# Four graph layers on 32 graphs: constants' set-up behind the first loads, zero fills and tables among the batches' operations, the last two batches' ends side by side

## The chip, the core and the metric

The kernel runs on one core of one Trainium2 chip, as one launch. The metric is the device time in microseconds (us). A core has five engines that run their own streams in order and meet at semaphores: TensorE (PE; its weight loads are listed as PEld), VectorE (DVE), ScalarE (ACT), GpSimd (POOL) and SyncE (SP), which issues the DMAs of the kernel before. Times of instructions come from a profile of one execution and are counted from the start of its span.

## The reference

The input `x` is 32 graphs of 512 nodes with 64 channels, `adj` is 32 weighted adjacency matrices of 512 by 512 in float32. Four layers follow each other, each with a residual and a layer norm:

```python
x = _layernorm(x + _L0_gnn_ref(x, adj), axis=-1)      # (A / deg) @ x
x = _layernorm(x + _L1_gnn_ref(x, adj, ...), axis=-1) # Chebyshev polynomials of the Laplacian, order 4
x = _layernorm(x + _L2_gnn_ref(x, adj, ...), axis=-1) # attention in hyperbolic space over all pairs of nodes
x = _layernorm(x + _L3_gnn_ref(x, adj, nodemask, ...), axis=-1)
```

The last layer thins the neighbours out (`_dilate_adj`), takes for each node and channel a weighted mix of the 0.25, 0.5 and 0.75 quantiles of its neighbours' values, and ends in a small network:

```python
sv = jnp.sort(vals, axis=2)            # neighbours' values, sorted for each channel
...
    q = gather(lo) * (1.0 - frac) + gather(hi) * frac
    agg = agg + wt * q
...
out = (1.0 + EPS_GIN) * x + agg
h = jax.nn.relu(jnp.einsum('bnc,ch->bnh', out, W1) + b1)
y = jnp.einsum('bnh,ho->bno', h, W2) + b2
return y * mask[..., None].astype(dtp)
```

## The kernel before

A batch is one graph; nodes are tiled as T = 4 tiles of P = 128 rows, D = 64 channels. The work of a batch is cut into lanes, each a function that records its operations: `front` (layers 0 and 1: four loads of the matrix as tiles `front_A`, transposes into `front_AT`, products), `pairs` (layer 2's pairwise part, tiles `EX`, `RW`, `Q`), `tail` (the end of layer 2 up to `x3`, sent to DRAM as `xs`), `graph` (the thinned matrix, ranks of the nodes by degree `rk`, slots of the neighbours), `gather` (the neighbours' values by one-hot products into the planes `SB` and `SH`), `sort` (a sorting network on `SB` for nodes from rank 32 on, then the products with the rank tables, collected in the PSUM tile `PA` and copied to `ap`), and, once for two batches, `head` (the network on `SH` for the first 32 ranks of both batches, sums in `PRS`).

`head` ends with `finish` for the one batch and then for the other. `finish` takes ranks back to nodes: it transposes `rk` (4 products with the identity), copies the result to `rr`, builds four one-hot tiles `PT` with two ACT operations each (`onehot`: an Abs with a bias into `dist`, then a Relu), multiplies `ap` by them, adds `x3`, and calls `dense`: two ACT copies (`oT`, `hT`) around the product with `w1s`, four pairs of products with `onesb` and `w2s`, then on DVE the mask and the residual, a layer norm (DVE statistics, a power on POOL, four ACT operations) and the DMA to `out`. The tiles `rr`, `oT`, `hT`, `zo` have one buffer and the lane has one PSUM bank `head_bank`, so that the second batch's end follows the first's.

The order is not that of the code. While `seq.on` is set, the class `Order` only records operations with costs written out by hand; `issue` (line 294) then plans them with due times by lane (`STAGES`) and tile buffers, and emits each engine's stream in the planned order. Where the plan leaves a gap on PE, it fills it with matmuls that compute nothing needed (`stay_active`, lines 1376 to 1379, into `PA`), one for each 0.11 us of the planned gap. They are real instructions: the stream runs through them whether the gap is there or not.

```python
if e == "PE":

    for _ in range(int((t - spare - fill) / 0.11)):
        before[e] = self.pin(filler(), before.get(e))
```

Ahead of this, the constants are set up in the usual way (lines 506 to 667): masks and index rows by POOL and DVE, eleven small loads and then the node mask on SP's queue (lines 589 to 643), products for folded weights into the PSUM pool `ps_0`. The masks' tile `nm` and the row `ii` share memory with tiles allocated later, so their users wait for one another. The table `tabs` is zeroed by POOL (line 555), filled by four DVE copies (lines 557 and 574). `SB`, `SH` and `PRS` are zeroed by POOL (lines 1368, 1369 and 1371). `PA` (line 1374) uses memory of `ps_0` and waits for the set-up's last product's copy, `b1f` (line 665). The first loads of the matrix stand behind the constants' loads on SP.

If a flag says that the degrees lie outside the planned bounds, a slow path (from line 1538) recomputes layer 3; it is not taken with these inputs.

Of the kernel before, what the change touches and what calls it, by code (L numbers as in the profile page):

```python
# [8 lines left out]
F32 = mybir.dt.float32  # L9
# [393 lines left out]
def tile_adj_resnorm(ctx: ExitStack, tc: tile.TileContext, x, adj, nodemask, w1k, b1k, att_w, att_b,  # L403
# [16 lines left out]
    pools = {}  # L420

# [79 lines left out]
    def bank(dtype=F32):  # L501
        return seq.tile(pools["ps"], [P, 512 if dtype == F32 else 1024], dtype, "bank", bufs=BANKS.get(seq.lane, 2))


# [20 lines left out]
    with tc.tile_pool(name="first", bufs=1) as first:  # L525
        ii = first.tile([P, N], I32, name="ii")
        nc.gpsimd.iota(ii, pattern=[[1, 2], [2, H2]], base=0, channel_multiplier=0)
        nc.vector.tensor_copy(iotap, ii)
# [21 lines left out]
    nc.vector.tensor_copy(kf, ks)  # L550
    tb = const.tile([P, K], F32, name="tb")
    ts(tb, kf, part, PAD, op0=OP.is_ge, op1=OP.mult)

    tabs = const.tile([P, K, P], F16, name="tabs")
    nc.gpsimd.memset(tabs, 0.0)
    for h in range(2):
        nc.vector.tensor_copy(tabs[h * HM:(h + 1) * HM, :, h * D:(h + 1) * D],
                              tb[h * HM:(h + 1) * HM].unsqueeze(2).to_broadcast([HM, K, D]))
    PADS, RANKS = slice(0, 2 * HM), slice(2 * HM, P)
    acc = const.tile([P, K], F32, name="acc")  # L560
    nc.vector.memset(acc, 0.0)
    tn = const.tile([P, K], F32, name="tn")
    tau = const.tile([P, 1], F32, name="tau")
    for q, w in TAUS:
        ts(tau, part, -1.0, q, op0=OP.add, op1=OP.mult)
        ts(tau, tau, 0.0, None, op0=OP.max)
        ts(tb, kf, tau, None, op0=OP.subtract)
        ts(tn, tb, -1.0, None, op0=OP.mult)
        tt(tb, tb, tn, op=OP.max)
        ts(tb, tb, -1.0, 1.0, op0=OP.mult, op1=OP.add)  # L570
        ts(tb, tb, 0.0, w, op0=OP.max, op1=OP.mult)
        tt(acc, acc, tb, op=OP.add)
    for h in range(2):
        nc.vector.tensor_copy(tabs[(h + 2) * HM:(h + 3) * HM, :, h * D:(h + 1) * D],
                              acc[(h + 2) * HM:(h + 3) * HM].unsqueeze(2).to_broadcast([HM, K, D]))
# [13 lines left out]
    nc.sync.dma_start(wk[:, :, :D], w1k.rearrange("k u c o -> (k u c) o").rearrange("(g p) o -> p g o", p=P))  # L589
    def rows(src, n, name, m):  # L590
        t = const.tile([m, n], F32, name=name)
        nc.sync.dma_start(t, bass.AP(tensor=src.tensor, offset=src.offset, ap=[[0, m], [1, n]]))
        return t

    def parts3(src, name):

        rem, n = src, src.shape[-1]
        full = const.tile([3, n], F32, name=name + "s")
        part3 = const.tile([3, n], BF16, name=name + "p")
# [12 lines left out]
    b1f = const.tile([3, D + 2], F32, name="b1f")  # L612
    nc.sync.dma_start(b1f[:, :D], bass.AP(tensor=b1k.tensor, offset=b1k.offset, ap=[[0, 3], [1, D]]))
    attb = rows(att_b, 1, "attb", P)
    bias2 = parts3(rows(b2, D, "b2f", 3), "bias2")
    meanf = const.tile([D, D], F32, name="meanf")
    nc.vector.memset(meanf, 1.0 / D)
    attw = const.tile([D, 2], F32, name="attw")
    for k in range(2):
        nc.sync.dma_start(attw[:, k:k + 1], bass.AP(tensor=att_w.tensor, offset=att_w.offset + (1 - k) * D, ap=[[1, D], [1, 1]]))  # L620
    b1c = const.tile([D, 1], F32, name="b1c")
    nc.sync.dma_start(b1c, bass.AP(tensor=b1k.tensor, offset=b1k.offset, ap=[[1, D], [1, 1]]))

    wt = const.tile([P, D], F32, name="wt")
# [8 lines left out]
    for h in range(2):  # L633
        nc.sync.dma_start(w1s[h * D:(h + 1) * D], w1)
    b1s = const.tile([HID, 1], F32, name="b1s")
    nc.sync.dma_start(b1s, b1.rearrange("(h u) -> h u", u=1))
    w2s = const.tile([HID, D], F32, name="w2s")
    nc.sync.dma_start(w2s, w2)

    nmask = const.tile([P, T, B], F32, name="nmask")  # L640
    with tc.tile_pool(name="ps_0", bufs=1, space=PSUM) as ps, tc.tile_pool(name="masks", bufs=1) as masks:
        nm8 = masks.tile([B, N], U8, name="nm8")
        nc.sync.dma_start(nm8, nodemask)
        nmf = masks.tile([B, N], F32, name="nmf")
# [10 lines left out]
        wkT = const.tile([D, P], F32, name="wkT")  # L655
# [573 lines left out]
    def head(b, res):  # L1229
# [22 lines left out]
        for g in range(2):  # L1252
            finish(b - 1 + g, res["ends"][g], ap[:, g])

    def finish(b, end, ap):
        rk, x3 = end
        pt = bank()
# [17 lines left out]
    def dense(po, x3T, x3, dst, nm):  # L1275

        fin = pools["fin"]
        oT = seq.tile(fin, [P, N], F32, "oT", 1)
# [5 lines left out]
        ph = bank()  # L1284
        mm(ph[:HID, :], w1s, oT, start=True, stop=True)
        hT = seq.tile(fin, [HID, N], F32, "hT", 1)
        act(hT, ph[:HID, :], AF.Relu, bias=b1s)
        py = bank()[:, :T * D].rearrange("p (t n) -> p t n", n=D)
# [3 lines left out]
        z = wide("zo")  # L1292
# [12 lines left out]
    gi = const.tile([P, B], I32, name="gi")  # L1305
    nc.gpsimd.iota(gi, pattern=[[-T, B]], base=0, channel_multiplier=1)
    gf = const.tile([P, B], F32, name="gf")
# [4 lines left out]
    def within_bounds():  # L1312
# [17 lines left out]
        for i, op in enumerate((OP.is_gt, OP.is_lt)):  # L1330
# [7 lines left out]

    STAGES = {"front": (-0.6, 0.2), "pairs": (1.2, 1.3), "tail": (0.2, 1.5), "graph": (0.9, 1.0), "gather": (2.7, 2.9),
              "sort": (4.5, 4.6), "head": (4.7, 5.6), "check": (3.1, 4.9)}

    nc.scalar.preload_act_table_set("natural_log_exp_and_others")
    with ExitStack() as fast:
        def pool(name, bufs, **kw):
            pools[name] = fast.enter_context(tc.tile_pool(name=name, bufs=bufs, **kw))
        pool("loads", 2)
# [4 lines left out]
        pool("keep", 2)  # L1353
        pool("oh", 2)
        pool("S", 1)
        pool("fin", 1)
# [9 lines left out]
        nc.gpsimd.memset(FLS[:, :, :, D + 1:D + 2], 1.0)  # L1366
        nc.gpsimd.memset(FLS[:, :, :, NL - 4:NL - 3], 1.0)
        nc.gpsimd.memset(SB, 0.0)
        nc.gpsimd.memset(SH, 0.0)
        PRS = pools["S"].tile([P, 2 * CUT * NR], F32, name="PRS")  # L1370
        nc.gpsimd.memset(PRS, 0.0)

# [250 lines left out]
```

## Time and profile before

| | |
|---|---|
| runs before | 2675.84, 2677.36, 2685.98 us; median 2677.36 us |
| profiled execution | 2680.23 us, span 2678.4 us |
| PE busy | 2514.1 us (94%), fillers among it |
| DVE busy | 2493.2 us (93%) |
| ACT busy | 1854.6 us (69%) |
| POOL busy | 352.9 us (13%) |
| DVE busy from 320 to 400 us | 79.10 of 80 us |
| DVE busy from 40 to 60 us | 6.59 of 20 us |
| DVE busy from 2640 to 2660 us | 2.07 of 20 us |
| mean granted TensorE clock | 0.98 |

The busy shares are averages over a start in which the lanes fill up, a long middle in which every batch goes through the same stream, and an end in which only the last two batches are left. In a list of the timeline, a line has the start in us, the length of the group in us, the engine, the source line, the operation, the output and inputs with their shapes, how many instructions were merged, and in brackets the idle time before it with what ended it. In the chain of waits a line has start, length, engine, tile or line.

### The profile page before, as it was taken

How to read it: one execution, taken by the hardware profiler on the slowest of the kernel's cores; microseconds unless marked ns; L12 is line 12 of the kernel's file. 1: busy time of each engine (PE TensorE's matmuls, PEld its weight loads, DVE VectorE, ACT ScalarE, POOL GpSimd, SP SyncE). 2: the span in 40 equal slices, each digit the busy share in tenths (PEclk: the TensorE clock that was granted, in tenths of full speed). 3: DMA queues.
4: the chain of work that ended last, by engine and by line, in shares of the span. 5: the costliest groups of instructions: out<-in, count | busy, mean ns of one | idle time of the engine just before them, and what ended most of it. 6: DMA issues, size and time to landing. Idle time of an engine off the chain costs nothing.

```text
span 2678.4 us, 55594 instructions
## 1 busy us (share of the span) xinstructions
PE 2514.1 (94%) x19764; PEld 1657.7 (62%) x19793; DVE 2493.2 (93%) x10191; ACT 1854.6 (69%) x4264; POOL 352.9 (13%) x329
## 2 busy tenths in 40 slices
PE   7999999999999999999999999999999999999988
PEld 5666566666666665665666666666566566666556
DVE  5689999999999999999999999999999999999993
ACT  2666768677677767777777776768767677776642
POOL 2111111111101111111111111111211111110100
PEclk9999999999999999899999999999999999999999
DMA  1100000000000000000000000000000000000000
GB/s 37 31 25 21 13 17 19 23 21 25 19 17 11 21 25 21 23 19 7 23 21 25 19 23 13 15 23 21 23 21 19 9 21 25 19 9 3 7 5 8
DMA packets 119721, 49.96 MB, mean 19 GB/s; under 512 B 53740, under 2 KB 119436, under 8 KB 119436
## 3 DMA queue, kind: packets, MB, share of 16 engines
q1 hardware_dynamic: 119436, 46.34, 6.5%
q8 instruction: 157, 2.57, 0.4%
q14 instruction: 128, 1.05, 0.1%
HBM read 37.93 MB, written 8.39 MB: 17 GB/s over the span
## 4 chain that ended last, share of the span: by engine, by line
DVE 74%; PE 18%; POOL 3%; ACT 2%; issue 2%; DMA 0%; POOLq 0%; DVEq 0%; ACTq 0%
DVE SB L445 17%; DVE SH L445 10%; DVE gather_oh L449 7%; PE front_bank L488 4%; DVE pairs_Q L445 3%; PE gather_bank L488 3%; PE pairs_bank L488 3%; DVE pairs_RW L445 3%; DVE pairs_Wt L452 2%; DVE pairs_L L452 2%; PE graph_bank L488 2%; PE head_bank L488 2%; DVE sort_prod L445 2%; DVE tail_v L445 2%; DVE pairs_EX L452 1%
## 5 line engine op out<-in xcount | busy, mean ns | idle before, releaser
L445 DVE TENSOR_TENSOR SB<-SB 128x448 f32<-128x448 f32 (+11 forms) x1424 | 573.6, 426 | 11.0
L488 PE MATMUL gather_bank<-gather_oh,tail_x3h 128*64 128x448 f16 (+2 forms) x5376 | 537.4, 332 | 4.3 <-ACT SB L469 3.7
L488 PEld LDWEIGHTS <-tail_x3h 128*64 128x64 bf16 x5376 | 303.2, 111 | 210.3 <-issue 107.9
L445 DVE TENSOR_TENSOR SH<-SH 128x128 f32<-128x128 f32 (+11 forms) x1744 | 358.3, 248 | 6.5
L488 PE MATMUL pairs_bank<-pairs_FT 67*128 67x512 f32 (+7 forms) x768 | 319.5, 519 | 19.6 <-DVE pairs_EX L452 13.8
L449 DVE TENSOR_SCALAR gather_oh<-graph_slot 128x256 f16<-128x256 f16 (+4 forms) x864 | 264.0, 352 | 10.7 <-PE gather_bank L488 10.6
L488 PE MATMUL front_bank<-front_AT,front_y 128*64 128x512 f32 x768 | 200.3, 615 | 13.0 <-DVE front_y L445 11.4
L694 POOL TENSOR_TENSOR front_rs<-front_var,mhalf 128x4 f32<-128x4 f32 x64 | 79.8, 1248 | 944.1 <-DVE front_var L449 815.8
L488 PEld LDWEIGHTS pairs_bank<-pairs_FT 67*128 67x128 f32 (+1 forms) x768 | 127.2, 195 | 78.4 <-DVE pairs_EX L452 22.2
L488 PEld LDWEIGHTS <-graph_nbT 128*128 128x128 f16 x1536 | 113.2, 99 | 82.0 <-DVE graph_do L452 23.5
L488 PE MATMUL PA<-identf,sort_prod 128*128 128x128 f32 (+4 forms) x960 | 151.0, 288 | 3.2 <-DVE sort_prod L445 2.5
L488 PE MATMUL graph_bank<-graph_perm,graph_V 128*128 128x512 f16 x512 | 135.9, 380 | 2.3 <-DVE graph_perm L449 2.0
L488 PEld LDWEIGHTS PA<-identf,sort_prod 128*128 128x128 f32 (+4 forms) x960 | 118.1, 173 | 26.7 <-issue 16.5
L488 PEld LDWEIGHTS pairs_bank<-FLS,pairs_Wt 128*128 128x128 f32 x1024 | 125.2, 192 | 14.6 <-DVE pairs_Wt L452 5.7
L469 ACT ACTIVATE graph_VP<-graph_bank 128x512 f16<-128x512 f32 x128 | 75.8, 592 | 76.8 <-PE graph_bank L488 76.2
L488 PE MATMUL pairs_bank<-FLS,pairs_Wt 128*128 128x66 f32 x1024 | 126.2, 273 | 2.0 <-DVE pairs_Wt L452 1.8
L488 PEld LDWEIGHTS front_bank<-XA,front_AT 128*128 128x128 f32 x1024 | 120.7, 192 | 9.2 <-ACT front_AT L469 3.0
L488 PE MATMUL front_bank<-XA,front_AT 128*128 128x65 f32 x1024 | 120.5, 273 | 0.8 <-ACT front_AT L469 0.6
L488 PE MATMUL head_bank<-head_PT,sort_ap 128*64 128x512 f32 x256 | 119.6, 616 | 0.6 <-ACT head_PT L469 0.6
L469 ACT ACTIVATE pairs_L<-pairs_L,pairs_oo 128x512 f32<-128x512 f32 x128 | 90.7, 719 | 40.9 <-DVE pairs_L L452 40.3
L469 ACT ACTIVATE graph_v<-graph_bank,graph_c 128x512 f16<-128x512 f32 x128 | 87.0, 680 | 43.0 <-PE graph_bank L488 22.6
L488 PE MATMUL graph_bank<-UC,graph_nbT 128*128 128x512 f16 (+3 forms) x512 | 93.7, 304 | 20.9 <-DVE graph_do L452 18.4
(327 smaller groups left out, 6169.4 us busy)
## 6 DMA issues: line engine op xcount, KB each, us to landing
front_A<-in_adj_dram SPq DMA_DIRECT2D x128, 256.0 KB, 2.8
XA<-in_x_dram SPq DMA_DIRECT2D x32, 128.0 KB, 2.2
xs<-tail_x SPq DMA_DIRECT2D x32, 128.0 KB, 2.0
out_dram<-head_zo SPq DMA_DIRECT2D x32, 128.0 KB, 2.0
wk<-in_L_gnn_weight_dram SPq DMA_DIRECT2D x1, 64.0 KB, 2.1
w1s<-in_L_gnn_W_dram SPq DMA_DIRECT2D x2, 32.0 KB, 2.2
attw<-in_L_gnn_att_W_dram SPq DMA_DIRECT2D x2, 0.2 KB, 2.3
w2s<-in_L_gnn_W_dram SPq DMA_DIRECT2D x1, 32.0 KB, 2.5
```

Source lines behind the costliest of these rows:

```text
L445: vec(lambda: nc.vector.tensor_tensor(out, a, b, op=op), out, [a, b])
L449: vec(lambda: nc.vector.tensor_scalar(out, a, s1, s2, op0=op0, **kw), out, [a], True, (s1, s2))
L452: vec(lambda: nc.vector.scalar_tensor_tensor(out, a, s, b, op0=op0, op1=op1), out, [a, b], False, (s,))
L469: 0.3, lambda: nc.scalar.activation(out, a, f, scale=scale, **kw), [out, accum_out], [a, after] + sc, table)
L488: return nc.tensor.matmul(out, w, a, start=start, stop=stop)
L694: seq.op("POOL", 0.8, 0.6, lambda: nc.gpsimd.tensor_tensor(y, v, mhalf, op=OP.pow), [y], [v])
```

## The change

1. The constants' loads are issued from ACT's queue in place of SP's, so that SP begins with the batches' loads. Set-up tiles that nothing later needs go into a pool `first` that is closed before the fast pools open, and the fast pools are opened in another order (`fin`, `oh`, `keep` first).
2. `SB`, `SH`, `PRS` and `tabs` are zeroed by ACT (a copy of a column of ones, scaled by 0, 768 columns at a time), and the tables are computed, as recorded operations in lane `gather` of batch 0; the four DVE copies into `tabs` become ACT copies.
3. The last two batches have their one-hot tiles built beforehand, in a lane `ends` of their own, in the memory of `EX` and `RW`; the last batch's end gets its own tiles (`ends`, in the memory of `Q`, and a column tile of lane `tail`) and the bank of lane `pairs`.

The streams of the built programs differ at their beginning and from the last batches' `gather` on; between them each engine's instructions stand in the same order in both. On PE the fillers behind each of the first four groups of transposes are 18, 18, 13 and 18 (12 each before); the 33 ahead of the first group stay.

```diff
+    setup = ctx.enter_context(ExitStack())
+    first = setup.enter_context(tc.tile_pool(name="first", bufs=1))
...
-    def bank(dtype=F32):
-        return seq.tile(pools["ps"], [P, 512 if dtype == F32 else 1024], dtype, "bank", bufs=BANKS.get(seq.lane, 2))
+    def bank(dtype=F32, home=None):
+        lane, seq.lane = seq.lane, home or seq.lane
+        t = seq.tile(pools["ps"], [P, 512 if dtype == F32 else 1024], dtype, "bank", bufs=BANKS.get(seq.lane, 2))
+        seq.lane = lane
+        return t
+    unit = const.tile([P, 1], F32, name="unit")
+    nc.vector.memset(unit, 1.0)
+    def fill(a):
+        for c in range(0, a.shape[1], 768):
+            z = a[:, c:min(c + 768, a.shape[1])]
+            act(z, unit.to_broadcast(list(z.shape)), AF.Copy, scale=0.0)
...
-    nc.gpsimd.memset(tabs, 0.0)
-    for h in range(2):
-        nc.vector.tensor_copy(tabs[h * HM:(h + 1) * HM, :, h * D:(h + 1) * D],
-                              tb[h * HM:(h + 1) * HM].unsqueeze(2).to_broadcast([HM, K, D]))
...
+    def tables():
+        ts(tb, kf, part, PAD, op0=OP.is_ge, op1=OP.mult)
+        for h in range(2):
+            act(tabs[h * HM:(h + 1) * HM, :, h * D:(h + 1) * D],
+                                  tb[h * HM:(h + 1) * HM].unsqueeze(2).to_broadcast([HM, K, D]), AF.Copy)
+        for q, w in TAUS:
...
+        for h in range(2):
+            act(tabs[(h + 2) * HM:(h + 3) * HM, :, h * D:(h + 1) * D],
+                                  acc[(h + 2) * HM:(h + 3) * HM].unsqueeze(2).to_broadcast([HM, K, D]), AF.Copy)
...
-    nc.sync.dma_start(wk[:, :, :D], w1k.rearrange("k u c o -> (k u c) o").rearrange("(g p) o -> p g o", p=P))
+    nc.scalar.dma_start(wk[:, :, :D], w1k.rearrange("k u c o -> (k u c) o").rearrange("(g p) o -> p g o", p=P))
...
-            finish(b - 1 + g, res["ends"][g], ap[:, g])
+            finish(b - 1 + g, res["ends"][g], ap[:, g], res["spots"][g] if b == B - 1 else None)
+    def spots(ends):
+        mid = pools["mid"]
+        seq.lane = "pairs"
+        home = seq.tile(mid, [P, 4, N], F32, "ends", 1, "Q")
+        ones = [seq.tile(mid, [P, 4, N], F32, f"ones{g}", 1, tag) for g, tag in enumerate(("EX", "RW"))]
+        seq.lane = "tail"
+        z = wide("ends", "u")
+        seq.lane = "ends"
+        for g, (rk, x3) in enumerate(ends):
+            pt = bank(home="pairs")
+            for t in range(T):
+                tr(pt[:, t * P:(t + 1) * P], rk[:, t:t + 1].to_broadcast([P, P]), identf)
+            act(home[:, 2], pt, AF.Copy)
+            for i in range(4):
+                act(home[:, 3], home[:, 2], AF.Abs, bias=nposc[:, i:i + 1])
+                act(ones[g][:, i], home[:, 3], AF.Relu, bias=1.0, scale=-1.0)
+        return [(ones[0], None), (ones[1], (home, z))]
+    def finish(b, end, ap, spot):
         rk, x3 = end
+        if spot:
+            ones, home = spot
+            po = bank(home=home and "pairs")
+            for u in range(2):
+                for h in range(2):
+                    mm(po[h * D:(h + 1) * D, :], ap[:, u, h * D:(h + 1) * D], ones[:, 2 * h + u], start=(u == 0),
+                       stop=(u == 1 and h == 1), pair=True)
+            for t in range(T):
+                mm(po[:D, t * P:(t + 1) * P], x3[:, t, :], identf, start=False, stop=(t == T - 1))
+            dense(po, None, x3, out[b:b + 1], nmask[:, :, b], home)
+            return
...
-    def dense(po, x3T, x3, dst, nm):
+    def dense(po, x3T, x3, dst, nm, home=None):
...
+        lane = home and "pairs"
+        oT = home[0][:, 0] if home else seq.tile(fin, [P, N], F32, "oT", 1)
...
-        z = wide("zo")
+        z = home[1] if home else wide("zo")
...
+    setup.close()
...
-        nc.gpsimd.memset(SB, 0.0)
-        nc.gpsimd.memset(SH, 0.0)
         PRS = pools["S"].tile([P, 2 * CUT * NR], F32, name="PRS")
-        nc.gpsimd.memset(PRS, 0.0)
...
         seq.on = True
+        seq.lane, seq.batch = "gather", 0
+        fill(tabs.rearrange("p k c -> p (k c)"))
+        tables()
+        for a in (SB, SH, PRS):
+            fill(a)
...
+            if b == B - 1:
+                both["spots"] = spots(both["ends"])
```

## The prediction

> **What bounds the kernel now.** I read the page's busy shares by slice, then the stretches, the chain of waits, and the timeline of the first 30 and the last 60 us.
>
> ```profile
> DVE  5689999999999999999999999999999999999993
> ACT  2666768677677767777777776768767677776642
> ```
>
> DVE, the row to watch, is full from the fifth of 40 slices (67 us each) to the last but one: in the middle DVE is the bound, and only the start and the end have room. In the start:
>
> ```profile
> 6.20 0.21 DVE L449 TENSOR_SCALAR identf<-diff 128x128 f32<-128x128 int32 x1
> ...
> 6.99 5.69 DVE L449 TENSOR_SCALAR bias2s<-bias2p,identf 3x64 f32<-3x64 bf16 x1
> ...
> 7.37 5.26 POOL L1368 MEMSET SB<- 128x6204 f32 x1
> ...
> 16.50 2.64 DVE L449 TENSOR_SCALAR gf<-gi 128x32 f32<-128x32 int32 x1
> ...
> 19.50 0.14 DVE L665 COPY b1f<-pw 3x2 f32<-3x2 f32 x1
> ...
> 26.13 0.60 PE L493 MATMUL front_bank<-identf,front_A 128*128 128x128 f32 x4
> ```
>
> Two DVE operations of the smallest size take 5.69 and 2.64 us; they end when POOL's zero fills of `SB` (7.37 to 12.63) and `SH` (16.04 to 19.10) end, while their like (`bias1s`, 0.24 us) take a tenth. `b1f` ends the set-up, and the first transposes come 6.6 us behind it, after 33 fillers. In the end, the chain of waits:
>
> ```profile
> 2634.68 0.55 PE head_bank L488 x4
> 2635.23 1.20 PE PA L1379 x10
> 2636.43 0.44 PE head_bank L493 x4
> 2636.87 3.06 PE PA L1379 x28
> ...
> 2653.43 0.44 PE head_bank L493 x4
> 2653.87 3.06 PE PA L1379 x28
> ...
> 2669.76 0.44 DVE head_zo L445
> ```
>
> Two equal ends, each about 17 us (2636.43 to 2653.43, then to 2669.76) with fillers (L1379) between every two steps. DVE is idle there (2.07 of 20 us from 2640 on). Nothing in the middle has room; 40 us of end and 26 us of start do.
>
> **The start.** The fills leave POOL, so the two stalls go: 5.69 - 0.24 and 2.64 less about 0.15, 7.95 us. From `identf` (6.20) to `b1f` (19.50) 13.30 us pass; 5.35 are left. In the changed stream nine small operations (`iotr`, `part`, the first `tb`, two `tau`) stand ahead of `b1f`; before, they took 21.65 to 23.05, 1.4 us. The node mask's cast, transposes and copy (0.41, 0.63, 0.28) now stand before the first `wkT`: 1.3. So 8.05 us from `identf` to `b1f`.
>
> When can `identf` start? DVE's operation before it needs `attw`. Before, that landed at 5.44. Now its second half shares a semaphore with the first `front_A` load, so ACT's queue waits for that landing: 0.75 (first issue) + 3.2 (median of these loads in the first 40 us) = 3.95; `b1c` to `nm` are queued behind it, and ACT's table load and fills behind them. That half then takes 2.3 alone (the `attw` loads of before), or 4.6, which the two `XA` loads took beside three matrix tiles: 6.25 to 8.55. I take the middle, 7.4; with 0.76 for product and subtraction (5.44 to 6.20), `identf` is at 8.15 and `b1f` at 16.2: gain 3.3 (2.15 to 5.25, the latter if `attw` is no later than before).
>
> [...]
>
> Then some is given back. Fillers among the first transposes are 67 in place of 48: 19 at 0.109 us (12 in 1.31 us): 2.07 lost. ACT's fills stand between its evictions of `front_AT`. An ACT copy of 640 columns takes 0.73 us, one of 256 0.38: 768 columns about 0.85, three 2.5, against 18 fillers and a group of transposes, 2.4 us: covered by PE's own fillers to 0.1 us a group, 0.3 in all at worst. After the last eviction some 4.6 us of fills and table copies follow on ACT, and DVE's next `tb` waits for them, with `front_deg` queued behind it. Their cover is PE's product (3.54 us) with 18 fillers ahead (1.96), 5.5 us less 0.6 for the eviction: 0.3 to spare; without it, each us late is one lost. The DVE casts into `tabs` (37.03 to 38.95, between `front_deg` and `front_dc`, on the chain) go: 1.92 gained, 0.5 back for some five small table operations at 0.1. The next two runs of fillers have 38 for 39, and `graph_do` covers the one before. Start: -3.3 + 2.1 - 1.9 + 0.5 = **-2.6 us**, between -4.6 (early `attw`) and -0.7 (late, with 0.3 and 0.5 for fills and table copies).
>
> The fills themselves, some 20 ACT operations, cost nothing more: ACT has 6.47 of 20 us busy from 40 on and waited 24.7 us for the first eviction. A shift of the start goes through whole, since the middle's streams are the same.
>
> **The middle's last part.** The one-hot tiles move ahead: two copies (0.60) and 16 operations (0.72 and 0.63 in turn), 12.0 us, into ACT's stream where it is busy 10.5 of 23 us (2533 to 2556). 22.5 of 23 fit barely. Queued behind them are evictions `graph_VP` and `graph_slot` and the squares of `tail`; DVE, which waits there only 0.34 us (for `tail_rnr`), would wait for those. Lowest 0, highest 2.7 (two Abs and Relu pairs before the last slot and the last square); I take one operation: **+0.8**.
>
> **The end.** Up to the copy of `head`'s part of `ap` (2635.71) the chain is as before: the 25 fillers ahead of the `PRS` transposes stay, and the earlier run of 29 is shorter, but DVE's `PRS` products hold that place. Then, in the changed order: 10 fillers, to 2636.3; six products by the one-hot tiles, in pairs on two column halves: four such of `front_y` side by side take 1.87 us, so 2.8 (apart, 1.0 each: 6.0), to 2639.1; eight of `x3` with the identity at 0.22 (two and four products took 1.88, the two 1.0): 1.8, to 2640.9. 10 fillers 1.1, to 2642.0, beside the two `oT` copies, done 2641.7. Two `w1s` products 2.0: 2644.0. Second `hT` 0.69: 2644.75, beside bias and 4 fillers. Eight bias and `w2s` pairs, four of which took 1.27: 2.5, to 2647.2. From there on one end took 8.64 (2669.76 to 2678.4). The second side by side adds four DVE operations, eight statistics and a bit (1.6, mostly beside), one more power on POOL (1.0) and four ACT operations behind the first four (1.43): +2.9. End 2658.7: **-19.7 us**. Best, with the second power and DVE's part wholly hidden (1.5 less added): -21.2; worst, products unpaired (+3.2) and layer norms one after the other (4.85 in place of 2.9): -14.6.
>
> **Sum.** -2.6 + 0.8 - 19.7 = -21.5 on the profiled execution's 2680.23 (span 2678.4). That one is 2.9 above the median of the runs; taken off the median 2677.36, **2656 us**. 0.5% is 13.4 us, about what a measurement of this kernel can tell from no change.
>
> **Rivals.** (1) The start gains nothing: constants land late under the matrix loads, fillers and fills eat the rest. For: 19 more fillers, the shared semaphore. Against: 7.95 us of stalls go. Start +0.5 in place of -2.6: 2659. (2) The ends are side by side in name only: PE takes the six products singly and ACT's crowding shows. For: one PE, one POOL, one ACT for both, and ACT full at 22.5 of 23. Against: the 164 fillers of the two ends (18 us at 0.109) become 14 whatever else happens. +3.2 +1.9 +1.9: 2663. (3) It does not do what it says: the first wait that decides lies in the last `sort` (95 fillers in place of 86 before a `sort_bank` product) and the end slides with it. 9 at 0.13 us (83 took 10.89) are 1.2 us, so it would need the end's gain gone too: no change. (4) Slower: the pools stand in another order, so that nearly every tile lies elsewhere in memory, and DVE, the bound, pays for its addresses. 21.5 us are 0.9% of DVE's 2493 us; it decides when a typical DVE operation is over 0.9% longer, 418 ns become 422; at 2% it is 2706. Against it: operations of one shape on ten different pairs of tiles now take the same:
>
> ```profile
> L445 DVE TENSOR_TENSOR tail_pr<-FLS,pairs_SS 128x256 f32<-128x256 f32 x32 | 13.4, 418 | 0.0
> L445 DVE TENSOR_TENSOR pairs_Q<-pairs_RW 128x256 f32<-128x256 f32 x32 | 13.4, 418 | 0.0
> ```
>
> **How the numbers follow.** Forecast 0.62; (1) 0.16; (2) 0.16; (3) 0.03; (4) 0.03. Faster by over 0.5% is the forecast, (1) and 0.13 of (2): 0.91. Same is (3) and the rest of (2): 0.06. Slower is (4): 0.03. All terms at their best give -25.8 (2651.6), all at their worst -11.2 (2666); the runs before spread from 1.5 below their median to 8.6 above. 8 in 10 lie in 2648 to 2664, which takes in (1) and most of (2).
>
> **What would show it.** Start: no DVE operation of some us in the first 20 us, `b1f` near 16, transposes near 23, the first product of `UC` near 37.5 for 40.1. Middle: DVE rows of one shape as long as before (rival 4 falls), DVE's wait under 1 us near the moved one-hot operations. End: from the last copy of `ap` to the end of the span 23 us in place of 42.7. I am wrong if the stretch from the last `sort_prod` to the end shrinks by less than 14 us, or if the middle's length changes by over 3 us.

## The result, and the profile after

The changed kernel takes 2654.29 us (median of 4 runs, 2648.0 to 2658.25) against 2678.47 us: ratio 0.9903, 95% interval 0.9875 to 0.9931. A second comparison, of five runs with nine of the kernel before, gave 2655.95 against 2683.16 us: 0.9898 (0.9883 to 0.9913). The profiled execution took 2658.25 us, with a span of 2656.5 us, 21.9 less than before. The forecast was 2656 us.

The busy shares by slice of the changed kernel:

```profile
DVE  3689999999999999899999999999999999999996
ACT  5666768677677777767777776867767677776861
```

DVE is now at work through most of the last slice (6 for 3), and ACT is busy from the first (5 for 2), with its fills. The start, from the timeline (start, duration, engine, line, operation, repetitions, and in brackets the idle time before it and what ended it):

```profile
7.41 0.21 DVE L451 TENSOR_SCALAR identf<-diff 128x128 f32<-128x128 int32 x1
8.20 0.23 DVE L451 TENSOR_SCALAR bias2s<-bias2p,identf 3x64 f32<-3x64 bf16 x1
...
14.92 0.15 DVE L683 COPY b1f<-pw 3x2 f32<-3x2 f32 x1 [0.28 <-PE pw L682]
...
15.93 5.57 PE L1426 MATMUL PA<-zero 128*128 128x256 bf16 x33
...
21.34 0.60 PE L495 MATMUL front_bank<-identf,front_A 128*128 128x128 f32 x4
...
35.96 0.72 PE L490 MATMUL graph_bank<-UC,graph_nbT 128*128 128x512 f16 x4 [0.50 <-DVE graph_do L454]
```

`bias2s` takes 0.23 us where it took 5.69, `b1f` is set at 14.92 for 19.50, the first transposes stand at 21.34 for 26.13, the first product of `UC` (in lane `graph`, the mark taken here for the end of the start) at 35.96 for 40.10: 4.1 us gained in these two profiles. The end, from the chain of waits:

```profile
2634.46 1.20 PE PA L1427 x10
2635.66 1.87 PE head_bank L490 x8
2637.52 0.86 PE pairs_bank L490 x4
...
2640.12 1.20 PE PA L1427 x10
2641.32 0.86 PE head_bank L490 x2
2642.18 0.89 PE pairs_bank L490 x3
...
2645.55 0.42 DVE head_zo L447
...
2648.76 1.02 POOL head_rs L712
...
2651.67 1.09 ACT tail_ends L471 x3
```

One end in place of two: products of both batches in turn (`head_bank`, `pairs_bank`), two runs of ten fillers (L1427), one layer norm's length. From the last copy of `ap` (2634.56 + 0.38) to the end of the span 21.56 us pass, 42.69 before: 21.1 gained.

That makes 25.3 (unrounded), but the two spans differ by 21.9. The difference of the same instruction's start in the two profiles shows where 3.4 us went:

| up to | before | after | difference |
|---|---|---|---|
| first product of `UC` | 40.10 | 35.96 | -4.1 |
| ninth copy of `front_sums` | 164.34 | 163.06 | -1.3 |
| 89th copy of `front_sums` | 2268.62 | 2266.08 | -2.5 |
| last row of `pairs_Q` | 2505.08 | 2502.63 | -2.5 |
| last copy of `ap` | 2635.33 | 2634.56 | -0.8 |
| end of the span | 2678.40 | 2656.50 | -21.9 |

2.9 us go between the first product of `UC` and 163 us, 1.7 in the last 130 us ahead of the end; the long middle between gives 1.2 back. In both places PE's granted clock is lower. The stretches by window (PE, PEld, DVE, ACT and POOL busy, then the clock, the DMA share and GB/s), first of the changed kernel, with the row of 24 products from the timeline, then of the kernel before:

```profile
120.00:130.00 10.00, 10.00 (x80) 9.12 (x80) 6.24 (x39) 7.73 (x28) 1.01 (x1) 0.73 0.20 55
2570.00:2580.00 10.00, 6.76 (x61) 4.31 (x59) 9.76 (x31) 2.37 (x4) 0.00 (x0) 0.98 0.01 2
2580.00:2590.00 10.00, 9.78 (x54) 5.07 (x55) 7.85 (x30) 5.67 (x11) 1.49 (x1) 0.68 0.00 0
...
2582.15 4.55 PE L490 MATMUL gather_bank<-gather_oh,tail_x3h 128*64 128x448 f16 x24
```

```profile
120.00:130.00 10.00, 9.29 (x89) 8.00 (x89) 7.17 (x43) 6.02 (x21) 2.19 (x2) 1.00 0.18 53
2580.00:2590.00 10.00, 6.99 (x57) 3.62 (x58) 9.90 (x37) 5.19 (x11) 1.05 (x1) 1.00 0.01 2
...
2583.70 2.46 PE L488 MATMUL gather_bank<-gather_oh,tail_x3h 128*64 128x448 f16 x24
```

The same 24 products take 4.55 us at a clock of 0.68 and 2.46 at 1.00, and DVE, busy 9.90 of these 10 us before, drops to 7.85 as it waits for them. A stretch of lower clock is called a dip from here on. Is this dip the change's doing, and if not, what did each part bring? The experiments ask that.

### The profile page after: what moved, and what is told of

Same layout as the page of the kernel before. It is cut to its first block, busy times and chain, and to the rows that moved or that the text cites. A ratio compares the mean times of both kernels' runs of the same rounds, so it can differ in the third digit from the quotient of the medians.

```text
span 2656.5 us, 55323 instructions
## 1 busy us (share of the span) xinstructions
PE 2494.8 (94%) x19626; PEld 1646.6 (62%) x19655; DVE 2476.7 (93%) x10187; ACT 1872.4 (70%) x4288; POOL 341.3 (13%) x325
## 4 chain that ended last, share of the span: by engine, by line
DVE 75%; PE 17%; POOL 3%; ACT 3%; issue 2%; DMA 0%; ACTq 0%; POOLq 0%; DVEq 0%
DVE SB L447 17%; DVE SH L447 10%; DVE gather_oh L451 7%; PE front_bank L490 4%; DVE pairs_Q L447 3%; PE pairs_bank L490 3%; DVE pairs_RW L447 3%; PE gather_bank L490 3%; DVE pairs_Wt L454 2%; DVE pairs_L L454 2%; PE graph_bank L490 2%; DVE sort_prod L447 2%; DVE tail_v L447 2%; PE head_bank L490 2%; DVE pairs_EX L454 1%
## 5 line engine op out<-in xcount | busy, mean ns | idle before, releaser
L490 PE MATMUL front_bank<-front_AT,front_y 128*64 128x512 f32 x768 | 201.4, 618 | 15.0 <-DVE front_y L447 13.4
L490 PEld LDWEIGHTS <-tabs 64*128 64x128 f16 x1296 | 49.6, 94 | 102.2 <-issue 96.1
L490 PE MATMUL head_bank<-head_PT,sort_ap 128*64 128x512 f32 x240 | 111.9, 621 | 0.6 <-ACT head_PT L471 0.6
```

Of the source, the lines that this page charges most:

```text
L490: return nc.tensor.matmul(out, w, a, start=start, stop=stop)
```

## The experiments

Each kernel was run with a profile and timed beside the kernel before; the kernels of one group of four share its runs. The marks of all profiles, us ("`UC` to 9th" is from the first product of `UC` to the ninth copy of `front_sums`, "last 130" from the last row of `pairs_Q` to the last copy of `ap`, "end" from that copy's end to the end of the span):

```
                        identf  b1f    transp. UC    9th copy  UC to 9th  last 130  end    ratio to before (95%)
before                  6.20    19.50  26.13   40.10  164.34    124.2     130.25   42.69
after                   7.41    14.92  21.34   35.96  163.06    127.1     131.93   21.56  0.9903 (0.9875-0.9931)
start alone             7.57    15.08  22.06   36.70  163.84    127.1     131.98   42.54  0.9985 (0.9975-0.9995)
ends alone              6.20    19.49  25.02   38.99  168.43    129.4     132.02   21.54  0.9923 (0.9901-0.9944)
places alone            6.20    17.37  23.25   35.27  161.57    126.3     132.10   42.58  0.9978 (0.9962-0.9995)
fills on POOL           10.75   19.20  25.35   39.68  163.95    124.3     132.20   21.50  0.9915 (0.9898-0.9931)
after, again            7.10    14.61  20.75   35.38  162.14    126.8     131.82   21.62  0.9898 (0.9883-0.9913)
constants on SP         6.07    13.58  19.37   34.00  161.15    127.2     131.97   21.54  0.9893 (0.9874-0.9912)
no fillers at start     7.31    14.83  15.83   33.49  161.13    127.6     131.83   21.45  0.9880 (0.9863-0.9896)
no fillers at end       7.26    14.77  21.58   36.21  163.36    127.2     132.24   21.09  0.9905 (0.9888-0.9921)
one-hots at their place 7.32    14.83  20.60   35.23  162.36    127.1     131.65   30.35  0.9948 (0.9931-0.9964)
one end after the other 7.38    14.90  20.44   35.07  162.37    127.3     130.63   25.43  0.9939 (0.9917-0.9960)
zeros in the set-up     6.88    13.67  16.77   31.41  156.48    125.1     130.51   20.45  0.9888 (0.9866-0.9909)
the same, fills later   6.08    13.06  16.20   29.32  155.53    126.2     130.51   20.63  0.9885 (0.9865-0.9905)
```

### The two halves of the change by themselves

Start alone is the changed kernel with the ends of before:

```diff
-            finish(b - 1 + g, res["ends"][g], ap[:, g], res["spots"][g] if b == B - 1 else None)
+            finish(b - 1 + g, res["ends"][g], ap[:, g], None)
...
-            if b == B - 1:
-                both["spots"] = spots(both["ends"])
```

> The start of the change alone (constants on ACT's queue, fills and tables among the batches' operations, the new order of the pools); the ends as before. Theory A (the start gained 4.1 us up to the first product of UC, 40.10 to 35.96, and what was lost behind it, 3.4 us up to the last copy of ap, came from dips of the granted clock that fell in places where PE is the bound and that lie elsewhere in each run): the first UC product stands at 36.0 within 0.3; the time is 4 us below before, ratio near 0.9985; what is left of the 4.1 us at 2500 us differs from the changed kernel's by what the clock table shows. Theory B (the loss is the change's own, through tile places or through the fills' tail on ACT): the gain is down to 1.5 us by 160 us again, with full clock there, and the time is within 1 us of before.

Ends alone is the kernel before with `bank`, `spots`, `finish`, `dense` and the stage `ends` of the change.

> The ends of the change alone (one-hot tiles ahead, second end with its own tiles and bank); the start as before. Theory A: the first UC product stays at 40.1; from the last copy of ap to the end of the span 21.6 us for 42.7; time 21 us below before, near 2657, ratio 0.992. If the one-hot operations crowd ACT (the forecast's +0.8, at most 2.7), the stretch from a DVE pairs_RW near 2504 to the last copy of ap is longer than before's 131.5 us by that much at full clock; Theory A has it longer by nothing but clock dips. Rival: the ends need the start's new tile places to be fast, then the end is over 25 us.

Measured: 2678.84 against 2683.37 us for the start (ratio 0.9985, some 4 us) and 2663.21 for the ends (0.9923, some 21 us). The product of the two ratios is 0.9908, beside 0.9903 and 0.9898 for the whole: the halves add up. The start's mark is 0.4 beyond the 0.3 that the expectation allowed (36.70), and with the start of before the mark stands at 38.99 for the 40.1 expected. Both have one reason. The 33 fillers ahead of the first transposes begin at half pace (one each 0.213 us and later one each 0.109, in the profiles of before and after), and the pace rises at another moment in each profile, so that they take 5.80 us before, 4.70 with the ends alone, 5.57 after and 6.14 with the start alone. The traces' clock records, which begin with this rise, put it at 24.65, 22.39, 19.62 and 20.94 us. The gain at the first product of `UC` is thus 2.3 to 5.0 us, depending on the profiles that are compared; at `b1f`, ahead of the fillers, it is 4.4 to 4.9. The end alone takes 21.54 us, to 0.1 what it takes in the whole, so it needs nothing of the other half.

The last 130 us settle the forecast's +0.8. With the one-hot operations ahead they take 131.8 to 132.2 us (ends alone, after, after again), without them in start alone 131.98 and in places alone 132.10: nothing, to some 0.3 us. The kernel before's 130.25 comes from the one profile of the 14 with no dip near 2575, where the last gather runs. In the three last of the table the clock reads 0.83 there for one window of 10 us, and the stretch takes 130.5 to 130.6; with 0.66 to 0.77 it takes 131.7 to 132.2, with or without the new ends (places alone, with 0.83 there and 0.73 at 2620, too).

### Where tiles lie, alone

The kernel before with the set-up's tiles in the pool `first`, closed ahead of the stages, and the pools `fin`, `oh`, `keep` first:

```diff
+    first = setup.enter_context(tc.tile_pool(name="first", bufs=1))
...
-        nm8 = masks.tile([B, N], U8, name="nm8")
+        nm8 = first.tile([B, N], U8, name="nm8")
...
+        pool("fin", 1)
+        pool("oh", 2)
+        pool("keep", 2)
         pool("loads", 2)
```

> Only the places of the tiles change: the set-up tiles in a pool closed early and the new order of the pools; the streams are those of before. Theory A: 418 to 419 ns for DVE's 128x256 f32 products as before, the two stalled DVE operations (5.69 and 2.64 us) still there, first UC product at 40.1 within 0.5, time the same within what five rounds can tell, ratio 0.999 to 1.001. Rival (tile places cost DVE): at least one large DVE form longer by 1% or more, and 5 us or more on the time.

This expectation failed. Its premise that the streams stay was wrong for the set-up: with another order of allocation the node mask's cast and copy move ahead, and POOL's fill of `SB` waits longer. The timeline of this run:

```profile
10.91 5.27 POOL L1371 MEMSET SB<- 128x6204 f32 x1
11.00 5.20 DVE L537 CAST iotr<-ic 128x4 f32<-128x4 int32 x1
...
28.98 1.92 DVE L575 CAST tabs<-acc 32x1536 f16<-32x1536 f32 x2
...
30.23 3.68 PE L490 MATMUL front_bank<-XA,front_AT 128*128 128x65 f32 x32
...
35.27 0.72 PE L490 MATMUL graph_bank<-UC,graph_nbT 128*128 128x512 f16 x4 [0.29 <-DVE graph_do L454]
```

Both stalls remain, one of 5.2 us and one that now falls behind `b1f` (17.37) and takes 1.9 us, and the casts into `tabs` start at 28.98, ahead of the product that covers them, in place of 37.03 behind it. With two memory edits the first product of `UC` stands at 35.27, as early as with the whole new start (35.07 to 36.70 in the six profiles that have it unaltered). So the moves of constants, fills and tables to other engines were not needed for the 4 us; that they bring their own is the next question. Of DVE's forms, the 128x256 products took 415 to 424 ns here, 413 to 417 in the changed kernel, 415 to 419 before: at most 1.4% up (`pairs_Q`, 424 for 418), on rows of 13.4 us, no time that shows.

### Fills back on POOL, constants back on SP

```diff
-        for a in (SB, SH, PRS):
-            fill(a)
+        nc.gpsimd.memset(SB, 0.0)
+        nc.gpsimd.memset(SH, 0.0)
+        nc.gpsimd.memset(PRS, 0.0)
```

> The changed kernel with the zero fills of SB, SH and PRS back as POOL memsets in the set-up; constants still on ACT's queue, tables still among the batches' operations. Theory A (DVE's two stalls came from POOL's memsets beside them): DVE operations of some us are back in the first 20 us, in all 5 to 8 us of them, b1f near 20 to 22 for 14.92, the first UC product 4 to 6 us later than 35.96 less what ACT's relief gives (up to 1). Rival (the stalls came from the constants' loads or their queue): no DVE operation over 1 us, b1f near 15, first UC product at 36 or earlier.

```diff
-    nc.scalar.dma_start(wk[:, :, :D], ...)
+    nc.sync.dma_start(wk[:, :, :D], ...)
```

> The changed kernel with the constants' loads back on SP's queue, ahead of the first matrix loads; every other stream identical. Theory A (the queue gains nothing, since the first transposes wait for PE and not for the matrix): attw lands about 5.4 again, identf near 6.2 for 7.41, b1f 1 us earlier than 14.92 or the same, first transposes and first UC product the same as the changed kernel's or up to 1.2 earlier (21.3 and 36.0); ratio as that of the changed kernel within 0.001. Rival (the matrix loads must stand first): first transposes 2 us or more later than 21.3, as the matrix lands behind the constants.

The timeline of the run with the fills on POOL:

```profile
4.76 5.27 POOL L1419 MEMSET SB<- 128x6204 f32 x1
4.81 5.27 DVE L451 TENSOR_SCALAR wk<-wk 64x64 f32<-64x64 f32 x1
...
12.55 2.98 POOL L1420 MEMSET SH<- 128x3456 f32 x1
12.56 3.02 DVE L451 TENSOR_SCALAR last<-kf 128x64 f16<-128x64 f32 x1
...
19.20 0.15 DVE L683 COPY b1f<-pw 3x2 f32<-3x2 f32 x1 [0.28 <-PE pw L682]
```

The stalls follow POOL's fills: the DVE operation issued beside the fill takes as long as it (5.27 and 3.02 us, where the like take 0.2), two of `TENSOR_SCALAR` here and a `CAST` in the run before. `b1f` goes back to 19.20 (I had written 20 to 22), the first product of `UC` to 39.68. The stalls' cause is settled, and the rival (the loads) falls.

In the profiles, ACT's queue cost time. With the constants first on SP's queue, `identf` is at 6.07 for 7.1 to 7.6, `b1f` at 13.58 for 14.6 to 15.1, and the first product of `UC` at 34.00 for 35.1 to 36.7 (the six profiles of the table with the change's start as it is). The matrix loads, now behind, are issued from 7.16 us on (the median of such loads takes 2.7 us in the changed kernel), so they still land long before the transposes at 19.37. I had allowed up to 1.2 us; it is 1.0 to 1.5 at `b1f`, and 1.1 to 2.7 at the first product of `UC`, where the moment of the clock's rise is in it. The times (0.9893 and 0.9898) do not tell the two apart.

The fills' run also answers the question on the 2.9 us, with another surprise: it loses 3.7 us at the first product of `UC`, yet its ninth copy of `front_sums` stands at 163.95, within 2 us of the changed kernel's, and its span is the same (2656.7). From `UC` to the ninth copy it takes 124.3 us, as the kernel before does, and neither has a dip there. Every profile with a dip there takes 126.3 to 129.4. (The last of the table takes 126.2 without one, but its fills lie elsewhere.)

### The changed kernel again, and without its fillers

> The changed kernel again, for a second profile and more runs. Theory A (the shape of start and end is fixed, the difference behind the start is where the granted clock dips fall): first UC product 36.0 within 0.3, last copy of ap to the end of the span 21.6 within 0.4; from the first UC product to the ninth front_sums copy 124.2 us if no dip lies there (as in the kernel before and in the run with POOL's fills) and 2 to 5 us more with one (127.1 in the first profile); ratio to before 0.990 to 0.992. Theory B (the loss is the change's own): that stretch is 127 us also at full clock.

The same kernel, in a second profile, gives the same end (21.62) and a start 0.6 us shorter (35.38, for the 0.3 that I had allowed), but a dip in another place: the clock is 0.86 from 90 to 100 us and 1.00 from 120 to 130, where the first profile had 1.00 and 0.73. Followed matmul by matmul, the second profile is 0.6 us ahead at 56 us, 1.1 behind at 101, and 1.2 ahead again at 127 (55.98, 100.58 and 127.27 against 56.56, 99.51 and 128.44): the dips cost 1.7 and 2.2 us where they fall, in one and the same program. Theory B (the loss is the change's own) needs this stretch at full clock; the run with zeros in the set-up, below, which has the same streams behind its start, gives it: 125.1. So of the 2.9 us some 0.8 are the change's own, by this one profile, and some 2 are the dip's.

```diff
-                for _ in range(int((t - spare - fill) / 0.11)):
+                for _ in range(int((t - spare - fill) / 0.11) if t > 40.0 else 0):
```

> The changed kernel without the fillers of the first 40 planned us (about 175, the 33 ahead of the first transposes and the groups between the first products). Theory A (fillers on the path are lost time; they take 5.6 us ahead of the first transposes): transposes at about 15.8 for 21.34, first UC product about 5 us earlier than 35.96 (30 to 31.5), where ACT's fills then bound it. Rival (PE must be kept warm: the first fillers take 0.17 us each and the later ones 0.109, so a PE without them runs up to 1.5 times slower): products among the first 40 us longer by a third or more (3.68 us for the 32 of front_bank become 5 or more), and the first UC product only 2 us earlier or not at all.

The other run has `t < max(clock.values()) - 46.0` as its condition.

> The changed kernel without the fillers of the last 46 planned us (about 174). Theory A (only two runs of ten lie on the path of the end): from the last copy of ap to the end 20.7 for 21.56, and nothing else. Rival (PE slows when it is left idle): the matmuls of the last 12 us take up to 1.5 times as long (the eight products by the one-hot tiles 2.97 us become 4 or more), and the end is 2 to 4 us longer.

The timeline and a window of the run without fillers at the start:

```profile
15.83 1.06 PE L495 MATMUL front_bank<-identf,front_A 128*128 128x128 f32 x4
...
25.07 7.06 PE L490 MATMUL front_bank<-XA,front_AT 128*128 128x65 f32 x32 [1.61 <-issue]
...
24.00:34.00 10.00, 7.97 (x50) 7.64 (x51) 3.73 (x21) 5.30 (x7) 1.01 (x1) 1.00 0.09 26
```

The transposes start 5.5 us earlier and take 1.06 us for 0.60; the product of `front_bank` takes 7.06 for 3.68. Of 5.5 us 1.6 to 3.2 are left at the first product of `UC` (33.49 for 35.1 to 36.7): the rival was right. The clock column reads 1.00 all the while: it does not show this state at the start, the durations do, for the trace's clock records begin with the rise, here at 45.10 us. The end gives 0.5 us (21.09 for 21.56), less than the 0.9 of theory A, for the same reason:

```profile
2632.00:2642.00 10.00, 6.57 (x35) 3.38 (x32) 2.39 (x9) 0.72 (x2) 0.00 (x0) 0.69 0.00 0
...
2636.36 2.88 PE L490 MATMUL head_bank<-pairs_ones,sort_ap 128*64 128x512 f32 x8 [0.53 <-ACT sort_ap L471]
```

This product row took 1.94 us behind fillers, where the same window reads 1.00.

### The end taken apart

```diff
+        if b == B - 1:
+            res["spots"] = spots(res["ends"], ap[P - CUT:, 0, 1, :])
+            seq.lane = "head"
...
-            act(home[:, 2], pt, AF.Copy)
+            act(home[:, 2], pt, AF.Copy, after=late)
```

> The changed kernel with the one-hot tiles of the last two ends made at their place, behind the last copy of ap, while the second end keeps its own tiles and bank. Theory A (18 ACT operations, 12.0 us, then stand between the copy and the second end's products): from the last copy of ap to the end of the span 27.5 us (26 to 29) for 21.56; time 6 us above the changed kernel's. Rival (side by side is what matters, the one-hots hide beside the other end's steps): under 24 us.

```diff
-        return [(ones[0], None), (ones[1], (home, z))]
+        return [(ones[0], None), (ones[1], None)]
```

> The changed kernel with the one-hot tiles made ahead, but both ends in head's one bank and tiles, one after the other. Theory A (an end without its one-hots is some 8.5 us up to its last product, and about 25 fillers stand in each again): from the last copy of ap to the end of the span 26 us (25 to 28) for 21.56. With the run before it this gives the shares: of the 21.1 us that the end gained, the one-hots ahead without the other part 16 to 17, side by side without the other part 15, the rest only together. Rival (nearly all comes from side by side): over 32 us.

One end after the other takes 25.43 us, near the 26 expected. One-hots at their place take 30.35, above the 26 to 29 that I had written: they pull the two ends apart again, so that the layer norms no longer lie side by side (`head_zo` is masked at 2642.61, `tail_ends` at 2648.29). So of the 21.1 us the one-hots ahead bring 17.3 by themselves (42.69 to 25.43), the second end's own tiles 12.3 by themselves (to 30.35; 15 expected), and 8.8 and 3.9 when added to the other.

### A faster version

```diff
+        def warm(n):
+            for _ in range(n):
+                nc.tensor.matmul(pd, zero[:, :P], zero, start=True, stop=True)
+        warm(18)
...
+                most = 10 if t < 5.0 else 4 if t > max(clock.values()) - 24.0 else 1000
```

> A try at a faster version: the changed kernel with the constants on SP's queue, 32 to 40 products of zeros in the set-up while PE has nothing to do, only 10 of the 33 fillers ahead of the first transposes, and at most 4 fillers at a place in the last 24 planned us. Theory A (a PE kept at work in the set-up runs its first products at full pace, so the fillers can go): first transposes at 16 to 16.5 (19.37 with the constants on SP's queue), 0.6 us for four of them, 3.7 us for the product of front_bank, first UC product at 30.5 to 31.5 (34.00); from the last copy of ap to the end 20.8 for 21.56. Rival (the zeros come too early and PE is slow again by 14 us): four transposes over 1 us, the product of front_bank over 5 us, first UC product later than 32. Ratio 0.988 to 0.9895.

```diff
+                if b == 0 and lane == "front":
+                    seq.lane = "gather"
+                    fill(tabs.rearrange("p k c -> p (k c)"), res["AT"])
+                    tables()
```

> As the run before it, and ACT's fills and the tables' casts only behind the first batch's evictions of front_AT, the tables' second part in a tile of its own. Theory A (ACT's fills between the evictions hold each back by some 0.65 us, and DVE's tb no longer waits for ACT): first UC product 2 to 3 us earlier than in the run before it, 28 to 29.5. Rival (the fills then stand ahead of the first copies of graph_v): the first front_sums copy is no earlier than in the run before it, and nothing is left of the gain.

PE's rows in the timeline of the first:

```profile
1.27 5.30 PE L668 MATMUL pd<-zero 128*128 128x256 bf16 x24 [1.27 <-DVE zero L605]
...
14.67 2.26 PE L1435 MATMUL PA<-zero 128*128 128x256 bf16 x10
16.77 0.60 PE L496 MATMUL front_bank<-identf,front_A 128*128 128x128 f32 x4
...
25.84 3.68 PE L491 MATMUL front_bank<-XA,front_AT 128*128 128x65 f32 x32
```

With zeros in the set-up and ten fillers, transposes and product run at full pace (0.60 and 3.68), and the first product of `UC` is at 31.41. The margin is small: the zeros end at 8.6 us, the clock is at half again from 13.32 to 16.73 us (so that the ten fillers take 2.26 us, for the 1.09 of ten at full pace), and the transposes start at 16.77. In the second run it stays at half until 18.44, and the first four transposes take 1.06 us again:

```profile
16.20 1.06 PE L496 MATMUL front_bank<-identf,front_A 128*128 128x128 f32 x4
```

With the fills behind the evictions the first product of `UC` is at 29.32, and the first copy of `front_sums` at 38.40 for 40.38, so that the rival falls there; at the ninth copy 1.0 of the 2.1 us are left. At the ninth copy of `front_sums` they are 5.7 to 7.5 us ahead of the changed kernel's two profiles, and the ends take 20.5 and 20.6. Their medians are 2648.9 and 2649.2 us; by ratio (0.9888 and 0.9885) they are not told apart from the changed kernel's 0.9898, since the intervals overlap, nor from the run that only leaves out the fillers at the start (0.9880).

## Why the prediction was right, step by step

The time lies 2 us from the forecast, and the mechanism held: the start gains what it gains through POOL's stalls and the casts, the end through the one-hots ahead and the ends side by side. That it is only 2 us is partly luck. By the runs the terms are -4.1 for the start, +0.8 behind it, 0 for the one-hots and -21.1 for the end, -24.4 in all for the forecast's -21.5; that agrees with the product of the halves' ratios (0.9908, 24.7 us of 2683). Start and end were both under-estimated, by 1.5 and 1.4 us, and the +0.8 written for the one-hots was met by the +0.8 behind the start, which stood in no term. Beside that, the median from which I counted, 2677.36, lies below those of the three later comparisons (2680.43 to 2683.37), and the profiled execution had no dip in two places where nearly all others have one.

Two places in the working are wrong without bearing on the forecast. All terms at their worst add up to -12.6 (-0.7, +2.7 and -14.6), not to the -11.2 written; and DVE's row reads 9 from the fourth slice on, not the fifth.

**The start, -2.6, was -4.1.** From the first transposes to the first product of `UC` the working held: 2.1 - 1.9 + 0.5 = +0.7 against a measured 14.62 - 13.97 = +0.65. The mis-sized terms are ahead of it: `identf` at 7.41 for 8.15, and 7.51 us from there to `b1f` for 8.05. The latter came out shorter by 0.5, and `attw`'s product starts at 6.95, not 7.4. Its second half is issued at 4.06, when the first matrix load has landed (4.04), as the working had it (3.95); the load then took 2.8 us, nearer to the 2.3 of a load alone than the 3.45 in the middle that I took. With the constants ahead on SP it is issued at 3.04 and the product starts at 5.61, so most of the 1.3 us is the wait in ACT's queue. A second issuing queue did not keep the constants as early as they were when they went first. It shows best in `wk`, issued at 0.74 and 0.75 us: its load takes 3.1 us beside the matrix loads and 2.0 ahead of them. Last, how long the fillers take ahead of the first transposes depends on the clock's rise, which was in no term: 0.2 us in favour of these two profiles, up to 1.4 between others with one and the same start.

**That 7.95 us of stalls would go** was right, and their cause too. What I did not see is that the order of memory alone moves one of the stalls and the casts off the chain, for as much gain.

**Fills and tables on ACT cost nothing more:** nearly. One fill took 0.76 us (3.02 for four) for the 0.85 of the working. The two later casts into `tabs` (2.97 us at 41.94) stand ahead of the first copy of `front_sums`, at 44.93 for 47.88 before, so that 3.0 of the 4.1 us are left there and, at full clock, 0.8 stay lost at the ninth copy.

**The middle, +0.8, was 0 to within 0.3**: the one-hot operations fit into ACT's gaps, and the trace shows no wait of DVE there (2528 to 2560 us). Most of what was lost behind the start (2 of 2.9 us, and the last 1.7) came from something that was in no term, the clock's dips. My sign that "the middle's length changes by over 3 us" counted as proof against the forecast. From the first product of `UC` to the last copy of `ap` it fired (2598.6 us for 2595.2), and it proved nothing, for the same streams, from the 9th to the 89th copy of `front_sums`, took between 2093.6 and 2104.3 us in the 14 profiles.

**The end, -19.7, was -21.1.** To the second product with `w1s` each step came out within 0.2 us of its term (first product 0.65 behind `ap`'s copy for 0.59, six paired products 2.6 for 2.8, eight with the identity 1.7 for 1.8). The mis-sized terms are the eight bias and `w2s` pairs, which began under the second `hT` and not behind it, so that the mask starts 10.6 us behind `ap`'s copy for 11.5, and the layer norms, 10.95 us for 8.64 + 2.9.

**The rivals.** (1) is wrong as put: the start gains, though in this profile a dip takes half of it back within 160 us. (2) is wrong: the products of both batches are paired, the ends lie side by side, and ACT's crowding costs nothing that shows; one after the other they would have taken 3.9 us more. (3) fell with the end. (4) fell: 413 to 417 ns for 415 to 419.

## What to carry to other kernels

Before moving work between engines to clear a start, look at which tiles of the set-up share memory with later ones: closing a pool early and another order of the pools did as much as all the moves together. Do not put a long POOL fill beside the small DVE operations of a set-up (here one of 0.2 us took 5.27), and let a PE that is about to be needed do zeros in the time that it has anyway, rather than when its first product could already start; here that showed in the profiles (the first four transposes took 0.60 us, for 1.06 with neither zeros nor fillers), not in the times. When two profiles are compared at a tenth of a per cent, look first at the clock by windows: here 1 to 3 us sat in dips that the same program has elsewhere in the next run.

## What the runs showed of the hardware

Without fillers at the start, PE was busy for 5.75 of the 10 us from 14 us on and ran its products at about half pace: 1.06 us for 0.60, 7.06 for 3.68. The dips agree in size and lie on a grid: in the 14 profiles every stretch of low clock ahead of the last 20 us reads 0.50, lasts 3.41 us or two to five times that, and starts a whole number of 3.41 us after the others of its profile (in the changed kernel the first two start at 118.60 and 500.90 us, 112 times 3.413 apart). The dip at 118.60 us in the changed kernel follows a window of 3.41 us in which PE was busy for 2.76:

```profile
115.19:118.60 3.41, 2.76 (x25) 2.48 (x23) 1.65 (x9) 0.08 (x1) 0.00 (x0) 1.00 0.00 0
118.60:125.43 6.83, 6.83 (x38) 6.42 (x38) 5.15 (x35) 3.16 (x10) 2.01 (x2) 0.50 0.00 1
125.43:128.84 3.41, 3.41 (x40) 3.06 (x39) 0.87 (x3) 3.41 (x15) 0.00 (x0) 1.00 0.50 132
```

In the second profile the window ahead of the dip at 97.25 has 2.74. Over all 14 profiles, 83 of 84 such windows at full clock with PE busy for under 1.5 us are followed by one at half clock, 126 of 443 with 1.5 to 2.5 us, 65 of 2084 with 2.5 to 3.2, and none of the 7645 with more. So a dip came with idle time of PE in the window just ahead of it, and 0.65 us of it was enough here. In the two profiles of the changed kernel the grid lies otherwise against the program (118.60 and 97.25 us are 6.3 times 3.41 us apart), and its dips lie in other places. What decides between two windows with gaps of one size stays open. The two shortest middles (2093.6 and 2095.6 us) are those with the least low clock (54.6 and 71.7 us, for 78.5 to 95.6 in the others).

With the fills on POOL, a zero fill held a DVE operation of 0.2 us for as long as the fill took (5.27 us for 5.27, 3.02 for 2.98), and beside the second fill the three behind it for 2.7 to 2.9; beside ACT's first four fills of `SB` in the changed kernel (13.06 to 16.08 us) no DVE operation took over 0.28 us.
